# An output bias written into PSUM by ScalarE in place of products with ones, and attention masks held in bf16

## The chip, the core and the metric

One NeuronCore of a Trainium2 chip runs the whole program. The metric is the device time of one launch in microseconds (us), as the median of three runs. TensorE is called PE in the views, its weight loads PEld, VectorE DVE, ScalarE ACT, GpSimd POOL and SyncE SP.

## The reference, cut to what matters

128 graphs of 128 nodes with 512 features each go through two layers. `adj` (int32) masks both attentions.

```python
# layer 0: attention with 8 heads of 64, then a projection with a bias
q, k, v = x @ Wq + bq, x @ Wk + bk, x @ Wv + bv
logits = where(adj > 0, q @ k.T / 8, -1e9)          # per head
out = softmax(logits) @ v
x = layernorm(x + relu(out @ Wo + bo))
# layer 1: graph attention with one head
Wh = x @ W1
e = leaky(Wh @ a1 + (Wh @ a2).T)                    # one column plus one row
attention = softmax(where(adj > 0, e, -9e15))
x = layernorm(x + leaky(attention @ Wh))
```

The change touches the `bo` of layer 0 and the masks of both layers.

## The kernel before, in words

**Turns.** The loop at L914 makes one turn `t` for each graph, software-pipelined: turn `t` computes the scores of graph `t` (`Softmax.scores`, L496), applies the softmax to them, and attends for graph `t-1` (`attend`, L573). Graphs are taken in pairs for the projections: in an odd turn, `LayerZero` (L649) multiplies the pair `(t-3)//2` by Wo; in an even turn, `LayerOne` (L739) multiplies a pair by W1. Groups of four graphs are multiplied by Wq, Wk and Wv (`group_product`, L349), in 21 steps that are spread over four turns by the calls `group()`. In turn `t` an `Edge` (L760) does the attention of layer 1 for graph `t-7`. The order on every engine is the order in which the code issues, since the schedule is manual (L840). The last four graphs, and all that is still in flight, follow a list written out by hand (`PLAN`, L1124), in which `a0.p1` is the method `p1` of the job `a0`; `a0`, `a1` and `a2` are the last three LayerZero pairs, `e0` to `e10` edges and `s0` to `s3` softmaxes.

**Pair products.** All the large products are made by Strassen's method: seven products `p1` to `p7` (numbered 0 to 6 as `n`) of half size go into three PSUM banks, called y, w and x, and the blocks of the result are read out of these as soon as they are complete (`strassen`, L294; the order is at L284). Each product is two multiplications in float32 (`multiply`, L444, one for each half of the contraction) of a 128-column stationary operand with 256 moving columns; the trace shows every such multiplication in float32 as two instructions, so a product is a row x4. For LayerZero, before the first product into bank y (`p1`) and the first into bank w (`p5`), one more multiplication (L447) puts the bias into the bank: `ones` (96 x 128, bf16) by half of `bias_rows` (96 x 512, bf16), in which the rows 0, 32 and 64 hold three bf16 parts that add up to `bo`. The second half of these rows holds the difference of the two halves of `bo`, as Strassen's sums need it. `load_bias` (L173) makes these rows in the turns at the start: one subtraction, and three times a cast, a copy of one row and a subtraction, all on VectorE, as "chores" that the calls `group()` take from a list.

**PSUM.** The banks of `psum()` (L98) rotate through five buffers of one tag (L95): a tile takes the buffer of the tile allocated five places earlier and has to wait until that one has been read. A turn allocates eight: the two score tiles `lg`, `p_e` (`Edge.turn`, L773), `p_y`, `p_w`, `p_x`, `p_oT` (`attend`) and `p_h` (`Edge.product`, L800). The banks of the group products are three others (L356).

**Masks.** `load_mask` fetches the int32 block, `mask_float` (L477) casts it to float32 on ScalarE, and `mask` (L482) turns it into 0 or -1e30 on VectorE. It is added to the scores (`Softmax.add`, L508, one instruction for each `lg` tile), and seven turns later `Edge.turn` transposes it on TensorE into `p_e` (L777), after a transpose of a broadcast column of Wh (L776).

Of the kernel before, what the change touches and what calls it, by code (L numbers as in the profile page):

```python
# [8 lines left out]
F32 = mybir.dt.float32  # L9
# [15 lines left out]
def kernel(  # L25
# [53 lines left out]

    nc = tc.nc
    B, P, D = x.shape
    assert P == 128 and B % GROUP == 0 and D == 4 * P
# [13 lines left out]
    def psum(name):  # L98
        return ps_mm.tile([P, D], F32, name=name, tag="mm")


    ident = const.tile([P, P], F32, name="ident")
    make_identity(nc, ident)
    mhalf = const.tile([P, 1], F32, name="mhalf")
    nc.gpsimd.memset(mhalf, -0.5)

# [45 lines left out]
    w1 = const.tile([P, 7, 2, HALF + 1], F32, name="w1")  # L152
    wv = dram.tile([7, P, 2, HALF], F32, name="wv", bufs=1)

    bias_rows = const.tile([96, D], BF16, name="bias_rows")
    nc.gpsimd.memset(bias_rows, 0.0)
    ones = const.tile([96, P], BF16, name="ones")
    nc.gpsimd.memset(ones, 1.0)

    def load_wv():  # L160

# [9 lines left out]
        return [write(0)] + ops + [write(n) for n in (4, 5, 1, 6, 3, 2)]  # L171

    def load_bias():  # L173

        bo_b = work.tile([P, D], F32, name="bo_b", tag="y")
        nc.sync.dma_start(bo_b, bo.partition_broadcast(P))
        ops = [lambda: nc.vector.tensor_sub(bo_b[:, HALF:], bo_b[:, HALF:], bo_b[:, :HALF])]

        def part(n):
            def split():  # L180
                row = slice(32 * n, 32 * n + 1)
                part = work.tile([P, D], BF16, name="b_part", tag="z")
                nc.vector.tensor_copy(part, bo_b)
                nc.vector.tensor_copy(bias_rows[row, :], part[row, :])
                nc.vector.tensor_sub(bo_b, bo_b, part)

            return split

        return ops + [part(n) for n in range(3)]

    def load_w1():

# [246 lines left out]
    def pair_product(xs, w, add, bias=None, home=None, bank=None):  # L439


        width = w.shape[-1]

        def multiply(p, n, start):  # L444
            if start and bias is not None and n in (0, 4):
                cols = slice(0, HALF) if n == 0 else slice(HALF, D)
                nc.tensor.matmul(  # L447
                    p[:, :width], ones, bias[:, cols], start=True, stop=True, skip_group_check=True
                )
                start = False  # L450
            for kc in range(2):
                nc.tensor.matmul(  # L452
                    p[:, :width],
                    xs()[n][:, kc, :],
                    w[:, PLACE[n], kc, :],
                    start=start and kc == 0,
                    stop=True,
                    skip_group_check=True,
                )

        def read_out(name, p, o):
            t = home(name) if home else work.tile([P, HALF + 1], F32, name=f"pr_{name}")
            nc.scalar.copy(t[:, :width], p[:, :width])  # L463
            return t[:, :width]

        return strassen(
            bank or (lambda role: psum(f"p_{role}")),
            multiply,
            read_out,
            lambda h, o, p, t: add(h, o, p[:, :width], t),  # L470
        )

    def load_mask(b):
        MF[b] = small.tile([P, P], I32, name="adj", bufs=2)
# [1 line left out]

    def mask_float(b):  # L477
        a = MF[b]
        MF[b] = small.tile([P, P], F32, name="mf", bufs=9)
        nc.scalar.copy(MF[b], a)  # L480

    def mask(b):  # L482
# [2 lines left out]
    class Softmax:  # L485
# [10 lines left out]
        def scores(self):  # L496
            b = self.b
            q, k = (a[b // GROUP, b % GROUP // 2] for a in (Q, K))
            cols = slice(b % 2 * P, (b % 2 + 1) * P)
            self.lg = [psum(f"lg{r}").rearrange("p (c k) -> p c k", c=NC) for r in range(2)]  # L500
            for c in range(NC):
                for r in range(2):
                    rows = slice(r * HD, (r + 1) * HD)
                    nc.tensor.matmul(  # L504
                        self.lg[r][:, c, :], q[rows, c, cols], k[rows, c, cols], start=True, stop=True
                    )

        def add(self, r):  # L508
# [64 lines left out]
        def attend(self):  # L573

            b = self.b
            v = V[b // GROUP, b % GROUP // 2][:, b % 2, :]
            self.oT = psum("p_oT").rearrange("p (c q) -> p c q", c=NC)
            for c in range(NC):
                for r in range(2):
                    h = 2 * c + r  # L580
                    nc.tensor.matmul(  # L581
                        self.oT[r * HD : (r + 1) * HD, c, :],
                        v[:, h * HD : (h + 1) * HD],
                        self.paT[:, r * NC + c, :],
                        start=True,
                        stop=True,
                    )

        def copy(self):
# [59 lines left out]
    class LayerZero:  # L649


        def __init__(self, pair, homes=None, on_scalar=False):
            self.pair = pair
            self.on_scalar = on_scalar
            self.homes = homes or {}
            self.y = self.norms = None
            self.d = {}
            pieces = pair_product(lambda: pair_blocks(OT, pair, "oS")[0], wo, self.add, bias_rows)
            for name, piece in pieces.items():
                setattr(self, name, piece)  # L660

# [98 lines left out]
    class Edge:  # L760
# [12 lines left out]
        def turn(self):  # L773
            self.s = WH[self.b][:, :, HALF : HALF + 1]
            self.p = psum("p_e").rearrange("p (c k) -> p c k", c=NC)
            nc.tensor.transpose(self.p[:, 0, :], self.s[:, 0, :].to_broadcast([P, P]), ident)  # L776
            nc.tensor.transpose(self.p[:, 1, :], MF.pop(self.b), ident)  # L777

        def add(self):
            self.e = self.tile("e", [P, P], small, 1)  # L780
# [68 lines left out]
    zero = {}  # L849
# [64 lines left out]
    for t in range(-3, END):  # L914
# [28 lines left out]

        last, sm = sm, Softmax(t) if on(t) else none
        sm.scores()
        while later:
            later.pop(0).go_back()
        if t < 3:
# [173 lines left out]
    for n in range(6):  # L1122
# [12 lines left out]
        v.c12 s2.exp.2.3 el.store s3.scores e0.maxima s2.exp.6.7 s1.fetch sl.attend e0.exp  # L1135
        s2.exp.4.5 e0.divide e1.turn b1.p5 s0.transpose sl.copy e0.product m3.cast
        s2.reciprocals.1 sl.sum.0 e1.add m3.mask b1.p2 s3.add.0 s2.divide.6.7 sl.sum.1
        s1.transpose s2.divide.4.5 a0.p1 sl.sum.2 b1.t2 e0.copy sl.sum.3 b1.p7 b1.c11 a0.t0
        s3.add.1 s2.exp.0.1 a0.p6 s3.reduce b1.t3 s0.attend a0.t2 e0.residual s3.exp.0.1 a0.p7
        s3.exp.6.7 a0.p5 b1.c22 x2.x a0.t3 s2.reciprocals.0 e1.maxima s3.exp.2.3 a0.p4  # L1140
        s2.divide.0.1 a0.c22 b1.p3 e1.exp s3.reciprocals.0 s2.divide.2.3 a0.c21 a0.p3 e1.divide
        s3.divide.0.1 s2.store a0.stats.1 e1.product s3.divide.2.3 b1.c12 a0.rstd.1 s3.exp.4.5
        s1.attend e0.stats e1.copy e3.turn s3.reciprocals.1 e0.rstd b1.p4 s0.copy e1.residual
        s2.fetch s1.copy a0.p2 e1.stats x3.x s3.divide.6.7 a0.c11 s1.sum.0 a0.c12 s3.divide.4.5
        s1.sum.1 e3.add s3.store a0.stats.0 s1.sum.2 e0.apply a1.p1 b1.c21 e1.rstd e0.store
        e3.maxima a0.apply.1 e2.turn a1.p2 a1.t0 a0.store.1 s2.transpose e3.exp a0.rstd.0 a1.p6
        e2.add s3.fetch e1.apply e2.maxima a1.p5 s1.sum.3 a1.t2 a0.apply.0 e3.divide a1.p7
        e1.store e2.exp a1.c11 a0.fetch.1 s2.attend e2.divide a1.t3 a1.c22 a1.p4 s2.copy
        a0.store.0 s3.transpose a1.p3 a1.c21 a1.stats.1 s3.attend a0.transpose.1 a0.fetch.0
        a1.rstd.1 e3.product s3.copy a1.c12 e2.product e3.copy a1.stats.0 s3.sum.0 a2.p2  # L1150
        a1.apply.1 s3.sum.1 e3.residual e2.copy a1.store.1 a2.p5 s3.sum.2 a0.transpose.0 a2.p1
# [63 lines left out]
```

## Time and profile before

| what | value |
|---|---|
| median of three runs (lowest, highest) | 2464.59 us (2463.76, 2466.36) |
| the profiled execution, its own time | 2466.47 us |
| its span, first to last instruction | 2464.4 us |
| granted TensorE clock | 0.996 of full |
| busy share of the span: PE, DVE, ACT, POOL | 98%, 73%, 58%, 32% |
| instructions | 43800 |
| L447, bias into bank y and into bank w | 64 and 64 |
| L777, transpose of the mask | 128 |
| L480, cast of the mask on ACT | 128, 289 ns at the median |
| L483, mask to 0 or -1e30 on DVE | 128, 185 ns at the median |

The profile is of one execution. A row of the timeline gives the start from the beginning of the span, the duration, the engine, the line of the code, the operation, the tiles (output, arrow, inputs), the shapes and a count, and in brackets how long the engine had been idle before it and what ended that. [...] several are under way at once. How long one holds up the next is therefore read from start to start.

### The profile page before, as it was taken

How to read it: one execution, taken by the hardware profiler on the slowest of the kernel's cores; microseconds unless marked ns; L12 is line 12 of the kernel's file. 1: busy time of each engine (PE TensorE's matmuls, PEld its weight loads, DVE VectorE, ACT ScalarE, POOL GpSimd, SP SyncE). 2: the span in 40 equal slices, each digit the busy share in tenths (PEclk: the TensorE clock that was granted, in tenths of full speed). 3: DMA queues.
4: the chain of work that ended last, by engine and by line, in shares of the span. 5: the costliest groups of instructions: out<-in, count | busy, mean ns of one | idle time of the engine just before them, and what ended most of it. 6: DMA issues, size and time to landing. Idle time of an engine off the chain costs nothing.

```text
span 2464.4 us, 43800 instructions
## 1 busy us (share of the span) xinstructions
PE 2425.7 (98%) x13713; PEld 1996.7 (81%) x13713; DVE 1807.8 (73%) x3739; ACT 1441.2 (58%) x5206; POOL 788.8 (32%) x1197
## 2 busy tenths in 40 slices
PE   8899999999999999999999999999999999999997
PEld 6688888888888888888888888888888888888874
DVE  5667777777777777777777777777777777777788
ACT  2555556556655655565566556555655665566574
POOL 2223333323233233333232332333332323323325
PEclk9999999999999999999999999999999999999998
DMA  6544544445545445444444454444454444544443
GB/s 191 180 137 149 160 150 155 162 143 156 162 142 170 140 157 164 147 155 162 142 158 156 150 166 145 154 163 147 156 162 141 159 154 151 167 145 153 154 150 112
DMA packets 351112, 379.92 MB, mean 154 GB/s; under 512 B 38936, under 2 KB 255008, under 8 KB 350880
## 3 DMA queue, kind: packets, MB, share of 16 engines
q1 hardware_dynamic: 350016, 376.07, 47.4%
q8 instruction: 110, 1.80, 0.3%
q10 hardware_dynamic: 864, 1.05, 0.2%
q14 instruction: 122, 1.00, 0.1%
HBM read 240.91 MB, written 136.05 MB: 153 GB/s over the span
## 4 chain that ended last, share of the span: by engine, by line
PE 93%; DVE 2%; issue 2%; POOL 1%; ACT 1%; DMA 1%; SPq 0%; DVEq 0%; POOLq 0%; ACTq 0%
PE st_y L366 27%; PE p_y L452 17%; PE st_w L366 14%; PE p_w L452 9%; PE st_x L366 7%; PE lg L504 5%; PE p_oT L581 5%; PE p_x L452 4%; PE p_h L803 4%; PE p_e L776 1%; PE p_e L777 1%; ACT pa L533 0%; POOL rstd L632 0%; ACT pa L547 0%; PE p_y L447 0%
## 5 line engine op out<-in xcount | busy, mean ns | idle before, releaser
L630 POOL TENSOR_SCALAR ve<-mv 128x1 f32<-128x1 f32 x256 | 69.2, 270 | 1336.5 <-DVE mv L626 1328.8
L533 ACT ACTIVATE pa<-pa,nmax 128x128 f32<-128x128 f32 x1008 | 392.7, 393 | 42.5 <-DVE nmax L522 34.4
L547 ACT ACTIVATE pa<-pa,rs 128x128 f32<-128x128 f32 x1008 | 331.4, 395 | 30.0 <-DVE rs L543 30.0
L594 ACT ACTIVATE oT<-p_oT,b_cols 128x128 f32<-128x128 f32 x504 | 142.9, 366 | 197.3 <-PE p_w L452 194.7
L513 DVE TENSOR_TENSOR pa<-lg,mf 128x512 f32<-128x512 f32 x252 | 161.8, 683 | 97.9 <-PE lg L504 95.4
L343 ACT COPY st_t<-st_y 128x512 f32<-128x512 f32 x192 | 110.5, 576 | 155.5 <-PE st_y L366 155.5
L504 PEld LDWEIGHTS lg<-kT,qT 64*128 64x128 f32 x2048 | 124.2, 187 | 91.9 <-issue 91.9
L533 ACT ACTIVATION_READ_ACCUMULATOR pa<-pa,nmax 128x1 f32 x1008 | 191.4, 190 | 0.0
L632 POOL TENSOR_TENSOR rstd<-ve,mhalf 128x1 f32<-128x1 f32 x256 | 176.6, 690 | 21.3
L463 ACT COPY pr_t<-p_y 128x257 f32<-128x257 f32 (+1 forms) x375 | 137.1, 366 | 63.6 <-PE p_y L452 60.5
L568 DVE STREAM_TRANSPOSE paT<-paz 128x1024 f32<-128x1024 f32 x126 | 156.8, 1245 | 1.4 <-PE p_oT L581 0.4
L522 DVE TENSOR_REDUCE nmax<-pa 128x8 f32<-128x1024 f32 x126 | 153.7, 1220 | 4.4
L504 PE MATMUL lg<-kT,qT 64*128 64x128 f32 x2048 | 148.8, 285 | 0.0
L347 ACT ACTIVATE st_t<-st_y,b_cols 128x256 f32<-128x256 f32 x192 | 80.5, 470 | 114.8 <-PE st_y L366 114.8
L581 PEld LDWEIGHTS p_oT<-paT,v 128*64 128x64 f32 x2016 | 107.5, 136 | 45.1 <-issue 39.5
L581 PE MATMUL p_oT<-paT,v 128*64 128x128 f32 x2016 | 137.9, 279 | 3.2 <-DVE paT L568 3.2
L781 ACT ACTIVATE e<-p_e,wh 128x128 f32<-128x128 f32 x117 | 43.2, 369 | 156.3 <-PE p_e L777 156.3
L751 DVE TENSOR_TENSOR wh<-p_w,pr_t 128x257 f32<-128x257 f32 x122 | 51.5, 422 | 110.4 <-PE p_w L452 63.6
L452 PE MATMUL p_y<-w,x1T 128*128 128x257 f32 x496 | 128.5, 381 | 2.5 <-ACT wk L463 1.7
L452 PE MATMUL p_y<-wo,oS 128*128 128x256 f32 x504 | 129.5, 379 | 0.4 <-ACT pr_t L463 0.4
L452 PE MATMUL p_y<-wo,oT 128*128 128x256 f32 x504 | 129.5, 379 | 0.0
L366 PE MATMUL st_y<-wv_n,xS 128*128 128x256 f32 x512 | 124.6, 386 | 3.7 <-ACT pa L547 2.8
(205 smaller groups left out, 6021.1 us busy)
## 6 DMA issues: line engine op xcount, KB each, us to landing
pa_dram<-pa SPq DMA_DIRECT2D x126, 512.0 KB, 2.6
paz<-pa_dram SPq DMA_DIRECT2D x504, 128.0 KB, 2.7
wv_n<-wv SPq DMA_DIRECT2D x224, 256.0 KB, 2.9
x<-in_x_dram SPq DMA_DIRECT2D x128, 256.0 KB, 2.9
x_dram<-x SPq DMA_DIRECT2D x128, 256.0 KB, 2.3
xz<-x_dram SPq DMA_DIRECT2D x512, 64.0 KB, 2.0
xz<-in_x_dram SPq DMA_DIRECT2D x496, 64.0 KB, 2.2
out_dram<-z SPq DMA_DIRECT2D x120, 256.0 KB, 2.5
```

Source lines behind the costliest of these rows:

```text
L366: nc.tensor.matmul(p[:, m, :], lhs, rhs, start=start and m == 0 and kc == 0, stop=True, skip_group_check=True,)
L452: nc.tensor.matmul(p[:, :width], xs()[n][:, kc, :], w[:, PLACE[n], kc, :], start=start and kc == 0, stop=True, skip_group_check=True,)
L463: nc.scalar.copy(t[:, :width], p[:, :width])
L504: nc.tensor.matmul(self.lg[r][:, c, :], q[rows, c, cols], k[rows, c, cols], start=True, stop=True)
L513: nc.vector.tensor_add(by_head[:, r * NC : (r + 1) * NC], self.lg[r].rearrange("p c (b k) -> p c b k", b=4), mf.unsqueeze(1).to_broadcast( ...
L522: nc.vector.tensor_reduce(self.nmax, by_head, AX.XY, ALU.max, negate=True)
L533: nc.scalar.activation(self.pa[:, :, h, :], self.pa[:, :, h, :], AF.Exp, bias=self.nmax[:, h : h + 1], accum_out=self.sums[:, h : h + 1],)
L547: nc.scalar.activation(self.pa[:, :, h, :], self.pa[:, :, h, :], AF.Copy, scale=self.rs[:, h : h + 1])
L568: nc.vector.transpose(self.paT.rearrange("p h (a i) -> p a h i", i=32), self.paz.rearrange("p a (h k) -> p a h k", k=32),)
L581: nc.tensor.matmul(self.oT[r * HD : (r + 1) * HD, c, :], v[:, h * HD : (h + 1) * HD], self.paT[:, r * NC + c, :], start=True, stop=True,)
L594: nc.scalar.activation(OT[pair][:, c, h * P : (h + 1) * P], self.oT[:, c, :], AF.Identity, bias=b_cols[:, 1, c : c + 1],)
L632: nc.gpsimd.tensor_tensor(self.r, ve, mhalf, ALU.pow)
```

## The change

The rows `bias_rows`, the tile `ones` and the two products with it go. `bo`, broadcast to 128 partitions in float32, stays in SBUF (`bo_b`), with the same subtraction of its halves. Two new pieces, `by` and `bw`, each allocate one bank (y or w) and have ScalarE copy 128 x 256 values of `bo_b` into it; `p1` and `p5` then accumulate onto it (no multiplication of theirs has `start`), and only `p2`, into bank x, starts afresh. In the loop the two pieces are issued in odd turns straight after the scores, ahead of `Edge.turn`; in `PLAN` each stands immediately ahead of its `p1` or `p5`. The other users of the same buffers (scores, `attend`, `turn`) set `start` on the first multiplication of a bank alone. The mask is cast to bf16 instead of float32, and its transpose in `Edge.turn` is a plain multiplication with a bf16 identity, which VectorE copies from the float32 identity at the start.

```diff
+    ident_b = const.tile([P, P], BF16, name="ident_b")
+    nc.vector.tensor_copy(ident_b, ident)
...
-    bias_rows = const.tile([96, D], BF16, name="bias_rows")
-    nc.gpsimd.memset(bias_rows, 0.0)
-    ones = const.tile([96, P], BF16, name="ones")
-    nc.gpsimd.memset(ones, 1.0)
+    bo_b = const.tile([P, D], F32, name="bo_b")
...
     def load_bias():
-        bo_b = work.tile([P, D], F32, name="bo_b", tag="y")
         nc.sync.dma_start(bo_b, bo.partition_broadcast(P))
-        ops = [lambda: nc.vector.tensor_sub(bo_b[:, HALF:], bo_b[:, HALF:], bo_b[:, :HALF])]
-        def part(n):
-            def split():
-                row = slice(32 * n, 32 * n + 1)
-                part = work.tile([P, D], BF16, name="b_part", tag="z")
-                nc.vector.tensor_copy(part, bo_b)
-                nc.vector.tensor_copy(bias_rows[row, :], part[row, :])
-                nc.vector.tensor_sub(bo_b, bo_b, part)
-            return split
-        return ops + [part(n) for n in range(3)]
+        return [lambda: nc.vector.tensor_sub(bo_b[:, HALF:], bo_b[:, HALF:], bo_b[:, :HALF])]
...
         def multiply(p, n, start):
-            if start and bias is not None and n in (0, 4):
-                cols = slice(0, HALF) if n == 0 else slice(HALF, D)
-                nc.tensor.matmul(
-                    p[:, :width], ones, bias[:, cols], start=True, stop=True, skip_group_check=True
-                )
-                start = False
+            start = start and (bias is None or n == 1)
...
+        ready = {}
+        def biased(role, half):
+            def run():
+                ready[role] = psum(f"p_{role}")
+                nc.scalar.copy(ready[role][:, :HALF], bias[:, half * HALF : (half + 1) * HALF])
+            return run
+        def get_bank(role):
+            if role in ready:
+                return ready.pop(role)
+            return bank(role) if bank else psum(f"p_{role}")
...
+        if bias is not None:
+            pieces["by"], pieces["bw"] = biased("y", 0), biased("w", 1)
...
-        MF[b] = small.tile([P, P], F32, name="mf", bufs=9)
+        MF[b] = small.tile([P, P], BF16, name="mf", bufs=9)
...
-            nc.tensor.transpose(self.p[:, 1, :], MF.pop(self.b), ident)
+            nc.tensor.matmul(
+                self.p[:, 1, :],
+                MF.pop(self.b),
+                ident_b,
+                start=False,
+                stop=True,
+                skip_group_check=True,
+            )
...
         sm.scores()
+        if t % 2 == 1 and on(t - 3):
+            zero[(t - 3) // 2].by()
+            zero[(t - 3) // 2].bw()
...
-        s1.transpose s2.divide.4.5 a0.p1 sl.sum.2 b1.t2 e0.copy sl.sum.3 b1.p7 b1.c11 a0.t0
+        s1.transpose s2.divide.4.5 a0.by a0.p1 sl.sum.2 b1.t2 e0.copy sl.sum.3 b1.p7 b1.c11 a0.t0
```

The other five places of `PLAN` are changed in the same way (`a0.bw`, `a1.by`, `a1.bw`, `a2.bw`, `a2.by`).

More of the change, by code (lines that the diff above doesn't have):

```diff
@@ L464, in read_out @@
             return t[:, :width]
-        return strassen(
-            bank or (lambda role: psum(f"p_{role}")),
+        ready = {}
[8 more added lines that the diff above has]
+            return bank(role) if bank else psum(f"p_{role}")
+        pieces = strassen(
+            get_bank,
             multiply,
@@ L471, in pair_product @@
         )
+        if bias is not None:
+            pieces["by"], pieces["bw"] = biased("y", 0), biased("w", 1)
+        return pieces
     def load_mask(b):
@@ L504, in scores @@
                     nc.tensor.matmul(
-                        self.lg[r][:, c, :], q[rows, c, cols], k[rows, c, cols], start=True, stop=True
+                        self.lg[r][:, c, :],
+                        q[rows, c, cols],
+                        k[rows, c, cols],
+                        start=c == 0,
+                        stop=True,
+                        skip_group_check=True,
                     )
@@ L584, in attend @@
                         self.paT[:, r * NC + c, :],
-                        start=True,
+                        start=c == 0,
                         stop=True,
+                        skip_group_check=True,
                     )
@@ L657, in __init__ @@
             self.d = {}
-            pieces = pair_product(lambda: pair_blocks(OT, pair, "oS")[0], wo, self.add, bias_rows)
+            pieces = pair_product(lambda: pair_blocks(OT, pair, "oS")[0], wo, self.add, bo_b)
             for name, piece in pieces.items():
@@ L776, in turn @@
             nc.tensor.transpose(self.p[:, 0, :], self.s[:, 0, :].to_broadcast([P, P]), ident)
-            nc.tensor.transpose(self.p[:, 1, :], MF.pop(self.b), ident)
+            nc.tensor.matmul(
[3 more added lines that the diff above has]
+                start=False,
+                stop=True,
+                skip_group_check=True,
+            )
         def add(self):
@@ L1137 @@
         s2.reciprocals.1 sl.sum.0 e1.add m3.mask b1.p2 s3.add.0 s2.divide.6.7 sl.sum.1
-        s1.transpose s2.divide.4.5 a0.p1 sl.sum.2 b1.t2 e0.copy sl.sum.3 b1.p7 b1.c11 a0.t0
+        s1.transpose s2.divide.4.5 a0.by a0.p1 sl.sum.2 b1.t2 e0.copy sl.sum.3 b1.p7 b1.c11 a0.t0
         s3.add.1 s2.exp.0.1 a0.p6 s3.reduce b1.t3 s0.attend a0.t2 e0.residual s3.exp.0.1 a0.p7
-        s3.exp.6.7 a0.p5 b1.c22 x2.x a0.t3 s2.reciprocals.0 e1.maxima s3.exp.2.3 a0.p4
+        s3.exp.6.7 a0.bw a0.p5 b1.c22 x2.x a0.t3 s2.reciprocals.0 e1.maxima s3.exp.2.3 a0.p4
         s2.divide.0.1 a0.c22 b1.p3 e1.exp s3.reciprocals.0 s2.divide.2.3 a0.c21 a0.p3 e1.divide
@@ L1144 @@
         s2.fetch s1.copy a0.p2 e1.stats x3.x s3.divide.6.7 a0.c11 s1.sum.0 a0.c12 s3.divide.4.5
-        s1.sum.1 e3.add s3.store a0.stats.0 s1.sum.2 e0.apply a1.p1 b1.c21 e1.rstd e0.store
+        s1.sum.1 e3.add s3.store a0.stats.0 s1.sum.2 e0.apply a1.by a1.p1 b1.c21 e1.rstd e0.store
         e3.maxima a0.apply.1 e2.turn a1.p2 a1.t0 a0.store.1 s2.transpose e3.exp a0.rstd.0 a1.p6
-        e2.add s3.fetch e1.apply e2.maxima a1.p5 s1.sum.3 a1.t2 a0.apply.0 e3.divide a1.p7
+        e2.add s3.fetch e1.apply e2.maxima a1.bw a1.p5 s1.sum.3 a1.t2 a0.apply.0 e3.divide a1.p7
         e1.store e2.exp a1.c11 a0.fetch.1 s2.attend e2.divide a1.t3 a1.c22 a1.p4 s2.copy
@@ L1150 @@
         a1.rstd.1 e3.product s3.copy a1.c12 e2.product e3.copy a1.stats.0 s3.sum.0 a2.p2
-        a1.apply.1 s3.sum.1 e3.residual e2.copy a1.store.1 a2.p5 s3.sum.2 a0.transpose.0 a2.p1
+        a1.apply.1 s3.sum.1 e3.residual e2.copy a1.store.1 a2.bw a2.p5 s3.sum.2 a0.transpose.0 a2.by a2.p1
         a1.rstd.0 x5.x e2.residual b2.p1 a2.t0 a0.sum.0 a1.apply.0 a1.fetch.1 a2.p6 a2.c11
```

## The prediction

> **What bounds the kernel now.** I read the page first: shares of busy time, then the chain that ended last.
>
> ```profile
> PE 2425.7 (98%) x13713; PEld 1996.7 (81%) x13713; DVE 1807.8 (73%) x3739; ACT 1441.2 (58%) x5206; POOL 788.8 (32%) x1197
> ...
> PE 93%; DVE 2%; issue 2%; POOL 1%; ACT 1%; DMA 1%; SPq 0%; DVEq 0%; POOLq 0%; ACTq 0%
> ```
>
> TensorE is busy for 98% and makes 93% of the chain. The table of TensorE's waits, asked for 100 to 2360 us, has four entries, 5.1 us in all, each met once and all before 116 us. So in the loop nothing is waited for: eight turns take 150.64 us in every one of the 13 stretches that I measured by the starts of the score products. There a change is worth what it takes from or adds to TensorE's own stream; only in the first 116 us and after 2400 us do other engines set the time. The stream of one odd turn, TensorE's timeline:
>
> ```profile
> 1213.56 0.27 PE L776 MATMUL p_e<-ident,wh 128*128 128x128 f32 x1
> 1213.66 0.27 PE L777 MATMUL p_e<-ident,mf 128*128 128x128 f32 x1
> 1213.77 0.28 PE L447 MATMUL p_y<-bias_rows,ones 96*128 96x256 bf16 x1
> 1213.89 1.03 PE L452 MATMUL p_y<-wo,oT 128*128 128x256 f32 x4
> 1214.75 0.27 PE L447 MATMUL p_w<-bias_rows,ones 96*128 96x256 bf16 x1
> 1214.86 1.03 PE L452 MATMUL p_w<-wo,oS 128*128 128x256 f32 x4
> ```
>
> The rows overlap, so a product's price is not its 0.27 us but the step to the next start: 0.12 and 0.11 us here. Over all 128 bias products the step is 111 to 114 ns, 113 at the median; after L777 it is 109 ns.
>
> [...] load rows of L452 (float32) last 190 ns at the median, those of L447 (bf16) 98. [...] the nearest rows here (L463, PSUM to SBUF, 128x256) have 366 ns. I use the trace's.
>
> **The change, part by part.**
>
> *Bias products out of TensorE.* 128 x 113 ns = 14.5 us, of which 122 in the loop, 13.8 us. The steps around them stay: 216 ns for a float32 product whether a bias product or another follows, 109 after L777.
>
> *Two copies on ScalarE in each odd turn.* Each about 0.37 us; successive ScalarE rows overlap by 0.1, so both take 0.64 us. Where they land, from ScalarE's timeline:
>
> ```profile
> 1210.74 0.58 ACT L809 COPY z<-p_h 128x512 f32<-128x512 f32 x1 [0.27 <-PE p_h L803]
> 1213.97 0.37 ACT L781 ACTIVATE e<-p_e,wh 128x128 f32<-128x128 f32 x1 [2.65 <-PE p_e L777]
> 1214.95 0.37 ACT L463 COPY pr_t<-p_y 128x256 f32<-128x256 f32 x1 [0.61 <-PE p_y L452]
> ```
>
> They stand between the first two rows, in 2.65 us of idle time: done by 11.32 + 0.64 = 1211.96, while TensorE wants bank y at 1213.77. That is 1.8 us of cover; behind them in ScalarE's queue are L781, which has to wait for TensorE anyway, and the exponentials. Cost nothing; without cover 0.64 us in each of 61 odd turns, 39 us. I count a gain from ScalarE as excluded.
>
> *Banks.* With `by` and `bw` ahead of `p_e`, an odd turn allocates lg, lg, y, w, e, x, oT, h instead of lg, lg, e, y, w, x, oT, h. Five places back: `by` now waits for the last turn's x, `bw` for its oT, both read long before (oT by ScalarE itself, earlier in its queue). `p_e` waits for the last p_h, whose copy (L809) ends 2.2 us or more ahead of L776 in every loop turn. `p_h` now waits for bank y of its own turn, last read by VectorE at L666: over all odd turns that read ends 0.91 us or more ahead of L803, and 0.23 us goes from this as TensorE gets faster, which leaves 0.68. The next turn's scores wait for bank w as before. All cost nothing; a VectorE later by 0.7 us would begin to show at L803.
>
> *Mask product in bf16.* [...] But the product after it needs a float32 load, and the trace starts each load 2 ns after the product before it has started, so loads run one ahead only. [...] its row is 92 ns longer than a bf16 one. So the step stays between 92 + 2 and 113 ns: from 1.9 us gained (128 x 15 ns) to 0.5 us lost. I take 0[...]. `start` on fewer products changes no count of instructions: 0. The cast to bf16 on ScalarE and the mask on VectorE have the same elements and both engines wait for TensorE: 0. No row shows an addition with mixed types (L513, 683 ns now, two a turn); a gain reaches nobody, and a loss shows only from 3.5 us a turn on, since VectorE idles 1.48 and 1.39 us between them and the reads of bank y, on top of the 0.68: 0.
>
> *Setup.* The bf16 identity is one VectorE copy while VectorE waits until 4.68 us for x: hidden. Two POOL memsets go, also hidden. But the splitting of bo into rows goes too, and that was in somebody's way. VectorE, then TensorE:
>
> ```profile
> 56.39 0.43 DVE L183 CAST b_part<-bo_b 128x512 bf16<-128x512 f32 x1
> ...
> 60.08 0.69 DVE L185 TENSOR_TENSOR bo_b<-bo_b,b_part 128x512 f32<-128x512 f32 x1
> 60.69 1.28 DVE L513 TENSOR_TENSOR pa<-lg,mf 128x512 f32<-128x512 f32 x2
> ...
> 63.14 1.23 DVE L568 STREAM_TRANSPOSE paT<-paz 128x1024 f32<-128x1024 f32 x1
> ```
>
> ```profile
> 64.43 1.09 PE L581 MATMUL p_oT<-paT,v 128*64 128x128 f32 x16 [0.94 <-DVE paT L568]
> 65.82 1.96 PE L366 MATMUL st_y<-xS,wq 128*128 128x256 f32 x8 [0.30 <-ACT st_t L347]
> 71.53 1.99 PE L366 MATMUL st_y<-xT,wq 128*128 128x256 f32 x8 [0.73 <-ACT st_t L347]
> 78.80 1.09 PE L581 MATMUL p_oT<-paT,v 128*64 128x128 f32 x16 [1.82 <-DVE paT L568]
> ```
>
> Nine operations hold the mask additions up by 4.3 us, and VectorE has no gap from there to the paT that TensorE waits for. Without them paT is ready near 62.0 (its DMA lands at 60.8) where TensorE comes at 63.5, and the exponentials start 4 us earlier: the waits of 0.94, 0.30 and 0.73 go, 2.0 us. The fourth depends on the store and fetch of the softmax: divisions end near 68 instead of 70.5, the fetch lands near 74.6, VectorE has paT near 76.1, against 75.0 at which TensorE would come. What is late next is this DMA: 0.7 of 1.82 goes. Later waits (1.11, 0.48, 2.85 us up to 112 us) hang on the same chain and move with it. Gain 2.6 us; bounds 0 (a later wait takes it back) and 3.8 (all four).
>
> *Tail.* Here `by` and `bw` stand straight ahead of their products, with ScalarE's queue ahead of them. The worst, `a1.by`, comes after `e0.apply`:
>
> ```profile
> 2400.02 0.84 ACT L641 ACTIVATE z<-z,shift,rstd 128x512 f32<-128x512 f32 x1
> ```
>
> Its copy ends near 2401.1, while `p1` starts its work at 2399.05 now: 2.1 us late. Of this 1.07 us is covered, since TensorE idled so long before `p6` at 2402.22; `p7`, now at 2404.89, would then be 0.8 late behind `a1.bw`. `a0.by` and `a0.bw` cost 0.2 and 0.4 by the same reading, inside that same cover; `a2.bw` about 0.5, against an idle 0.88 us at 2415.57. I take a net 0.7 us lost, the six products saved there included; bounds 0.7 gained (all covered) and 2.5 lost (no cover).
>
> *Sum.* -13.8 - 2.6 + 0.7 + 0 = -15.7 us. The profiled execution took 2466.47 us, 2.1 around its span of 2464.4; the sum makes it 2450.8 (span 2448.7). It lies 1.9 above the median of the runs, 2464.59, and the saving is the same for both: **2448.9 us**.
>
> **The rivals.** *The mask product shrinks with its columns* (load not in the way): 128 x 53 ns = 6.8 us more, 2442.1. For it: bf16 loads and products are shorter. Against it: the float32 load behind it. *Only the stream gets shorter*: the start's 2.6 us is taken back by the next wait and the tail has no cover: -13.8 + 2.5, 2453.3. For it: at 105 to 116 us four other waits follow. *Slower: the copies become the wait of each odd turn.* If the bank's release reaches ScalarE only with TensorE's group step ahead of L776 (rows end at 1213.7), the copies are done at 1214.35 instead of 1211.96, bank y is late by about 0.7 us against a saving of 0.226, and 61 x 0.47 = 29 us makes 2493. It decides from 1.8 + 0.23 = 2.0 us of lateness on. Against it: nothing that these banks held is still read then. That the products with ones stay in some form is excluded by the diff.
>
> **How the numbers follow.** Forecast 0.74; shrinking mask 0.07; stream alone 0.12; late copies 0.07, of which 0.03 near break-even. Lower end: -13.8 - 0.7 - 3.8 - 1.9 = -20.2, 2444.4; upper: -13.8 + 0 + 0.5 + 2.5 = -10.8, 2453.8; runs lie up to 1.8 above their median, so I end the range at 2444.0 and 2455.0. Left out are the shrinking mask and the late copies, 0.14, and a little of the rest. 0.2%, 4.9 us, is about what a measurement of this kernel can tell from no change. Faster 0.93, same 0.03, slower 0.04.
>
> **What would show it.** Eight turns at 150.64 - 8 x 0.113 = 149.74 us; 128 ScalarE rows from bo_b, in loop turns ahead of L781's idle time; the mask product's step near 109 ns; TensorE's 0.94 us wait at 64 us gone; new waits of TensorE for ScalarE only after 2385 us. Wrong if eight turns are not near 149.7, or if TensorE waits for p_y or p_h in the loop.

## The result and the profile after

The changed kernel took **2455.38 us** at the median (four runs, 2454.73 to 2456.53) beside 2464.55 us for the kernel before (four runs, 2463.76 to 2466.36): a ratio of 0.9962, with a 95% interval of 0.9945 to 0.9980 (each experiment below has its ratio and, in brackets, the same interval). That is 9.2 us faster, where 15.7 had been forecast. The profiled execution after took 2454.73 us with a span of 2452.6. The page, first the shares of busy time, then the chain by engine:

```profile
PE 2412.3 (98%) x13585; PEld 1989.0 (81%) x13585; DVE 1802.0 (73%) x3731; ACT 1478.2 (60%) x5334; POOL 789.8 (32%) x1195
...
PE 93%; issue 1%; DMA 1%; DVE 1%; ACT 1%; POOL 1%; SPq 1%; DVEq 0%; POOLq 0%; ACTq 0%
```

TensorE has 128 instructions and 13.4 us of work less, ScalarE 128 more and 37 us more, and TensorE makes 93% of the chain as it did before. `bo` is zero in the inputs of all runs: they show what the copies cost in time, not that a product accumulated onto a copy gives the right sum. The page hides where the difference lies. So I cut both traces at two marks, the first score product of graph 8 and that of graph 124:

| stretch | before, us | after, us | difference | forecast |
|---|---|---|---|---|
| start, to graph 8 | 174.65 | 172.31 | -2.3 | -3.3 |
| loop, graph 8 to 124 | 2186.09 | 2173.60 | -12.5 | -13.1 |
| end, from graph 124 | 103.66 | 106.73 | +3.1 | +0.7 |
| sum (span) | 2464.4 | 2452.6 | -11.8 | -15.7 |

In the forecast column six of the 122 bias products (0.7 us) stand with the start, where they are. The two profiled executions differ by 11.8 us, the medians by 9.2.

**The loop.** TensorE's timeline of a turn, after (in the changed kernel L784 is the transpose of Wh, L785 the mask product, L435 a pair product):

```profile
1223.45 0.27 PE L784 MATMUL p_e<-ident,wh 128*128 128x128 f32 x1
1223.56 0.22 PE L785 MATMUL p_e<-ident_b,mf 128*128 128x128 bf16 x1
1223.62 1.09 PE L435 MATMUL p_y<-w,x1T 128*128 128x257 f32 x4
1224.54 1.03 PE L435 MATMUL p_w<-w,x1S 128*128 128x257 f32 x4
```

Eight turns take 149.75 us (150.64 before). The bias products are gone, and nothing waits in their place. But the mask product's step is now 56 ns, not 109; instead the pair product after it takes 0.92 us from start to start, where the next of its kind takes 0.87. For its first instruction alone the step is 272 ns instead of 219: 56 + 272 = 328 = 109 + 219.

**The start.** TensorE, after (L588 is `attend`):

```profile
63.20 1.09 PE L588 MATMUL p_oT<-paT,v 128*64 128x128 f32 x16
...
78.81 1.97 PE L588 MATMUL p_oT<-paT,v 128*64 128x128 f32 x16 [4.40 <-DVE paT L575]
```

At 63.20 it is 1.23 us earlier than before and waits for nothing; near 71.5 us it is 2.5 us ahead. Then it stands for 4.40 us and goes on at 78.81, where the kernel before went on at 78.80: all the lead is gone at one instruction. The DMA issues on SP's queue say why, first before, then after (L553 and L560 store the softmax, L559 and L566 fetch it back):

```profile
66.44 0.43 SPq L195 DMA_DIRECT2D a_b<-in_L_gnn_a_dram  x1
70.58 0.34 SPq L553 DMA_DIRECT2D pa_dram<-pa  x1
73.23 1.75 SPq L559 DMA_DIRECT2D paz<-pa_dram  x4
```

```profile
66.80 0.43 SPq L183 DMA_DIRECT2D a_b<-in_L_gnn_a_dram  x1
67.34 0.36 SPq L560 DMA_DIRECT2D pa_dram<-pa  x1
73.01 1.75 SPq L566 DMA_DIRECT2D paz<-pa_dram  x4
```

The store is issued 3.24 us earlier, but its fetch only 0.22 us earlier. From issue to landing the store took 5.6 us, where it takes 2.6 in most of the run. Just ahead of it stand the loads of layer 1's weights, 1.5 MB issued from 63.0 to 66.8 us. VectorE's mask additions felt it too; they need the buffer that the store reads:

```profile
73.08 1.29 DVE L520 TENSOR_TENSOR pa<-lg,mf 128x512 f32<-128x512 f32 x2 [4.14 <-DMA pa_dram<-pa]
```

**The granted clock.** Busy time by stretch, before and then after (the columns are the stretch, its length, busy time and instructions of PE, PEld, DVE, ACT and POOL, the granted TensorE clock, the DMA share and GB/s):

```profile
78.00:84.00 6.00, 5.20 (x45) 4.32 (x46) 3.70 (x14) 4.86 (x20) 1.01 (x2) 1.00 0.45 146
112.00:121.00 9.00, 8.06 (x23) 6.11 (x24) 3.79 (x6) 3.45 (x11) 5.03 (x7) 0.62 0.68 221
```

```profile
78.00:85.00 7.00, 6.19 (x34) 4.67 (x36) 4.70 (x15) 5.00 (x20) 2.00 (x3) 0.54 0.45 148
106.00:122.00 16.00, 11.50 (x72) 8.83 (x72) 10.83 (x20) 8.85 (x34) 9.06 (x10) 1.00 0.69 210
2387.00:2392.00 5.00, 4.33 (x13) 3.45 (x14) 4.62 (x12) 3.71 (x10) 4.36 (x11) 0.66 0.84 305
```

The kernel before had its low clock in 112 to 121 us, after its wait of 2.85:

```profile
112.27 2.40 PE L366 MATMUL st_y<-wv_n,xS 128*128 128x256 f32 x8 [2.85 <-ACT pa L547]
```

There it cost 9 x 0.38 = 3.4 us of full clock. The changed kernel has it in 78 to 85 (7 x 0.46 = 3.2 us), after the wait of 4.40, and once more in the end (5 x 0.34 = 1.7 us), at a place where the kernel before had none. Only in the last 13 us have both of them a low clock, after a wait of 3.15 us in each (13.3 us from that product to the end before, 13.2 after), so this makes no difference between them.

The values between 0.5 and 1 are means of stretches that are low in part. Cut at 0.1 us, the clock is 0.50 from 113.6 to 120.5 us before, and from 77.6 to 84.4 and from 2388.4 to 2391.9 after: 6.9, 6.8 and 3.5 us. So the start has as much low clock before as after, 3.4 us of full clock each; its loss is not a matter of the clock between these two profiles.

**The end.** TensorE, then ScalarE, after (L456 is the new copy, L649 the apply):

```profile
2377.95 1.13 PE L435 MATMUL p_w<-wo,oS 128*128 128x256 f32 x4 [1.00 <-ACT p_w L456]
2387.67 1.39 PE L435 MATMUL p_y<-wo,spare 128*128 128x256 f32 x4 [2.01 <-ACT p_y L456]
2401.47 1.10 PE L435 MATMUL p_w<-wo,oS 128*128 128x256 f32 x4 [0.56 <-POOL oS L264]
```

```profile
2386.47 0.86 ACT L649 ACTIVATE z<-z,shift,rstd 128x512 f32<-128x512 f32 x1
2387.18 0.43 ACT L456 COPY p_y<-bo_b 128x256 f32<-128x256 f32 x1
```

In the kernel before, TensorE had these waits there:

```profile
2402.22 1.10 PE L452 MATMUL p_y<-wo,spare 128*128 128x256 f32 x4 [1.07 <-ACT pr_t L463]
2404.89 1.10 PE L452 MATMUL p_y<-wo,spare 128*128 128x256 f32 x4 [0.59 <-POOL shift L637]
2415.57 1.14 PE L452 MATMUL p_y<-w,x1T 128*128 128x257 f32 x4 [0.88 <-DVE x1T L245]
```

The wait that the forecast foresaw is there, 2.01 us for `a1.by` behind `e0.apply` (forecast 2.1), with 0.17 and 1.00 for pair `a0`. What follows it was not foreseen: the low clock, 0.66 in the mean of 2387 to 2392 us.

### The profile page after: what moved, and what is told of

It reads as the page before. It is cut to its first block, busy times and chain, and to the rows that moved or that the text cites. A ratio compares the mean times of both kernels' runs of the same rounds, so it can differ in the third digit from the quotient of the medians.

```text
span 2452.6 us, 43635 instructions
## 1 busy us (share of the span) xinstructions
PE 2412.3 (98%) x13585; PEld 1989.0 (81%) x13585; DVE 1802.0 (73%) x3731; ACT 1478.2 (60%) x5334; POOL 789.8 (32%) x1195
## 4 chain that ended last, share of the span: by engine, by line
PE 93%; issue 1%; DMA 1%; DVE 1%; ACT 1%; POOL 1%; SPq 1%; DVEq 0%; POOLq 0%; ACTq 0%
PE st_y L354 27%; PE p_y L435 17%; PE st_w L354 14%; PE p_w L435 9%; PE st_x L354 7%; PE lg L506 5%; PE p_oT L588 5%; PE p_x L435 4%; PE p_h L818 4%; PE p_e L784 1%; DMA wv_n<-wv 0%; SPq L228 0%; ACT pa L540 0%; POOL rstd L640 0%; PE p_e L785 0%
## 5 line engine op out<-in xcount | busy, mean ns | idle before, releaser
L588 PEld LDWEIGHTS p_oT<-paT,v 128*64 128x64 f32 x2016 | 108.2, 137 | 46.8 <-issue 39.9
L588 PE MATMUL p_oT<-paT,v 128*64 128x128 f32 x2016 | 138.8, 280 | 5.0 <-DVE paT L575 5.0
L435 PE MATMUL p_y<-w,x1T 128*128 128x257 f32 x496 | 131.6, 388 | 1.6 <-ACT wk L446 1.5
L435 PE MATMUL p_y<-wo,oT 128*128 128x256 f32 x504 | 132.7, 386 | 0.2 <-ACT p_y L456 0.2
L435 PE MATMUL p_y<-wo,oS 128*128 128x256 f32 x504 | 129.4, 379 | 0.0
L435 PE MATMUL p_y<-w,x1S 128*128 128x257 f32 x496 | 128.0, 380 | 0.0
```

The costliest lines, as they stand in the source:

```text
L435: nc.tensor.matmul(p[:, :width], xs()[n][:, kc, :], w[:, PLACE[n], kc, :], start=start and kc == 0, stop=True, skip_group_check=True,)
L588: nc.tensor.matmul(self.oT[r * HD : (r + 1) * HD, c, :], v[:, h * HD : (h + 1) * HD], self.paT[:, r * NC + c, :], start=c == 0, stop=True, ...
```

## The experiments

Theory: the loop gave what was forecast, the mask nothing; the end lost more because of waits for copies and the low clock that the longest of them brings; the start lost because the store stands behind weight loads. Rivals: the mask gives something that is hidden; the loss in the end has nothing to do with the copies; the clock alone sets the start.

**The changed kernel again (r_same).** No edit.

> The changed kernel again, unaltered. Theory: the loop is fixed (eight turns at 149.75 us in nearly every stretch), and what differs between executions lies in the first 125 us and after 2385 us, where TensorE waits and its granted clock drops to about half for some 5 us at a time; so the median is 2455 to 2456 and the profile shows the drop at 79 to 85 us again or at another place. Rival (the loop itself varies, by a stray DMA or copy that is late): stretches of eight turns scatter by 0.3 us or more.

2456.68 us beside 2466.22: 0.9957 (0.9945 to 0.9970). The start took 172.59, the loop 2173.13 and the end 106.62 us, so the three differences repeat. The low clock came in the end again (0.66 in 2387 to 2392), but at the start in two places, behind waits of 3.19 and 2.71 us:

```profile
77.00:82.00 5.00, 4.80 (x27) 3.67 (x29) 3.03 (x13) 3.86 (x16) 0.68 (x1) 0.66 0.48 157
110.00:119.00 9.00, 7.66 (x21) 5.76 (x22) 4.15 (x7) 4.56 (x15) 4.53 (x6) 0.62 0.70 231
```

The loop in the profile after was longer by 0.47: TensorE waited once for a load of `wv_n` near 1460 us, and here it doesn't. The 116 bias products of the loop are thus worth 12.96 us, 0.112 each.

**The mask alone taken back to float32 (x1_mask_f32).** To hold memory, `bo_b` is bf16, so `bo` is rounded.

```diff
-        MF[b] = small.tile([P, P], BF16, name="mf", bufs=9)
+        MF[b] = small.tile([P, P], F32, name="mf", bufs=9)
...
+            nc.tensor.transpose(self.p[:, 1, :], MF.pop(self.b), ident)
```

> The changed kernel with its masks back in float32 and transposed as before (bo_b is held in bf16 to make room, which rounds bo). Theory (the float32 weight load behind the mask product sets the step, whatever the product takes): the step after the mask product is 109 ns instead of 56, the next product gives the 53 ns back, eight turns stay at 149.75 us, total within 1.5 us of the changed kernel, 2454 to 2457. Rival (bf16 masks are part of the gain): eight turns at 150.17, total 6.8 us above the changed kernel, 2462.

2454.91 beside 2466.22: 0.9951 (0.9937 to 0.9965). TensorE's rows have the old steps again, 0.11 us after the mask product:

```profile
1224.85 0.27 PE L786 MATMUL p_e<-ident,wh 128*128 128x128 f32 x1
1224.96 0.27 PE L787 MATMUL p_e<-ident,mf 128*128 128x128 f32 x1
1225.07 1.03 PE L437 MATMUL p_y<-w,x1T 128*128 128x257 f32 x4
```

Eight turns take 149.75 and the loop 2173.13 us, as in r_same; the end takes 107.10. The bf16 mask is thus worth nothing in the changed kernel; this is shown.

**No bias at all (x2_no_bias).** `by`, `bw` and their six places in `PLAN` go; `bo` is left out.

```diff
-            pieces = pair_product(lambda: pair_blocks(OT, pair, "oS")[0], wo, self.add, bo_b)
+            pieces = pair_product(lambda: pair_blocks(OT, pair, "oS")[0], wo, self.add)
```

> The changed kernel without any bias in layer 0's projection: no copies into PSUM, no products with ones (bo is left out). Theory (in the loop the copies are covered, in the last pairs they stop TensorE): eight turns stay at 149.75 us, TensorE's waits of 0.17, 1.00 and 2.01 us after 2370 us are gone with the half clock that follows, total 2.5 to 4 us below the changed kernel, 2451.5 to 2453. Rival (the copies cost something in each odd turn): eight turns fall below 149.6. Rival (the end loses its time to other waits): the last 107 us from the scores of graph 124 on stay as long as in the changed kernel.

2453.96 beside 2466.22: 0.9951 (0.9939 to 0.9964). The loop is 2173.13, the same to 0.01 us as with the copies: in the loop they cost nothing. In the end the waits for copies and the low clock are gone (granted 1.00 in 2370 to 2392 us), but the end is 105.61, only 1.1 shorter, less than expected. TensorE now waits 1.43 us for a read-out on ScalarE (`pr_t`), 1.54 for `x1T` on VectorE and 1.26 for `wk` on ScalarE. This suggests that a good part of the end is a chain of other engines that reappears wherever TensorE is relieved. The start is 170.91 here, with a low clock of 3.4 us alone (79.4 to 82.8), and none behind a wait of 2.62 us at 111.82.

**The mask product ahead of the transpose (x3_mask_first).** The mask product sets `start`, and the float32 transpose comes between it and the pair product.

```diff
-            nc.tensor.transpose(self.p[:, 0, :], self.s[:, 0, :].to_broadcast([P, P]), ident)
             nc.tensor.matmul(
                 self.p[:, 1, :],
                 MF.pop(self.b),
                 ident_b,
-                start=False,
+                start=True,
                 stop=True,
                 skip_group_check=True,
             )
+            nc.tensor.transpose(self.p[:, 0, :], self.s[:, 0, :].to_broadcast([P, P]), ident)
```

> The changed kernel with the two multiplications of Edge.turn exchanged: the bf16 mask product ahead of the float32 transpose. Theory (the float32 load behind the mask product is what hides its gain): now the transpose, with its shorter load, follows the mask product [...]; each turn is 53 ns shorter, eight turns 149.33 us, total 6.5 us below the changed kernel, 2449. Rival (going from bf16 to float32 costs a fixed 53 ns, or TensorE keeps a least distance between products): eight turns stay at 149.75 and the total at 2455.

2450.61 beside 2466.22: 0.9932 (0.9920 to 0.9945). TensorE's timeline:

```profile
1223.84 0.22 PE L784 MATMUL p_e<-ident_b,mf 128*128 128x128 bf16 x1
1223.90 0.28 PE L792 MATMUL p_e<-ident,wh 128*128 128x128 f32 x1
1224.01 1.03 PE L435 MATMUL p_y<-w,x1T 128*128 128x257 f32 x4
...
1224.88 1.03 PE L435 MATMUL p_w<-w,x1S 128*128 128x257 f32 x4
```

The steps are 56, 112 and 219 ns, the pair product takes 0.87 again, and eight turns take 149.33, 0.42 less (8 x 53 ns). So the gain of the shorter mask product is seen or hidden by what stands behind it, and neither a fixed price of the change from bf16 to float32 nor a least distance between products is the reason, since both orders have the change. That it is the float32 load of the pair product which hides the gain fits the load rows (190 ns for a pair product, 137 for the transpose), but is argued from them. The start of this profile is 175.59 us, with low clock in 77.0 to 83.9 and 111.2 to 121.5.

**The loads of W1 behind the store (x5_late_w1).** They are issued at the end of turn 1, the work on them a turn later.

```diff
-        if t == 1:
-            late_chores = load_w1()
-        if t in (0, 2):
+        if t in (0, 3):
...
+        if t == 1:
+            late_chores = load_w1()
```

> The changed kernel with the load of W1 issued at the end of turn 1 instead of at its start, behind the store and fetch of that turn's softmax; its VectorE chores start a turn later. Theory (the store of the softmax lands at 73 us before and after the change, because W1 and the row of a, 1.5 MB on the same queue, are ahead of it): the store issued at 67.3 us lands near 70, the paT that TensorE waits for comes 2 to 3 us earlier, its wait of 3.2 to 4.4 us at 78 us falls below 1.5 and the half clock behind it does not come; total 3 to 5 us below the changed kernel run beside before, by which the ratio to before falls to 0.9945. Rival (the store itself takes 5.6 us whatever is ahead of it): wait and total as in the changed kernel.

2456.20 beside 2465.07: 0.9966 (0.9953 to 0.9978), and the start 176.87, 4.6 longer. The first half is as expected: the store, issued at 66.89, is followed by its fetch at 69.52, and TensorE waits 1.22 instead of 4.40. So the loads ahead of it were what delayed the store. But 10 us later, TensorE and ScalarE:

```profile
75.21 1.09 PE L588 MATMUL p_oT<-paT,v 128*64 128x128 f32 x16 [1.22 <-DVE paT L575]
85.05 1.57 PE L435 MATMUL p_y<-wo,oT 128*128 128x256 f32 x4 [3.81 <-ACT p_y L456]
```

```profile
83.94 0.30 ACT L482 CAST mf<-adj 128x128 bf16<-128x128 int32 x1 [4.64 <-DMA adj<-in_adj_dram]
```

The load of `adj` now stands behind W1 on SP's queue (issued at 78.85), the cast of the mask waits for it, and the copy of the bias stands behind the cast on ScalarE. That is the hazard of the change: TensorE's product now waits for whatever is ahead of the copy in ScalarE's queue.

**The copies earlier in the end (x4_early_copies).** Each stands several entries ahead of its product in `PLAN`, `a1.by` ahead of `e0.apply`. Shortened:

```diff
-s2.divide.6.7 sl.sum.1 s1.transpose s2.divide.4.5 a0.by a0.p1
+s2.divide.6.7 a0.by sl.sum.1 s1.transpose s2.divide.4.5 a0.p1
-a0.c12 s3.divide.4.5 s1.sum.1 e3.add s3.store a0.stats.0 s1.sum.2 e0.apply a1.by a1.p1
+a0.c12 a1.by s3.divide.4.5 s1.sum.1 e3.add s3.store a0.stats.0 s1.sum.2 e0.apply a1.p1
```

> The changed kernel with by and bw of the last three pairs moved ahead in the written-out order, as far as the rotation of the banks allows (bw of the first and of the second pair and both of the third straight behind the allocation before them; by of the second pair only behind c12, which frees its bank at 2386.4 us). Theory (ScalarE's queue ahead of the copies is the wait): of TensorE's 3.2 us of waits for these copies about 1.2 are left, all for by of the second pair; with a wait that short the half clock may not come; 1.5 to 3 us less from the scores of graph 124 to the end than the changed kernel's 106.6. Rival (the banks come free late): waits as before the move.

2454.61 beside 2465.07: 0.9960 (0.9947 to 0.9974). The end is 104.83, 1.9 shorter. One wait for a copy is left, and the clock is 1.00 in 2375 to 2392 us:

```profile
2385.72 1.13 PE L435 MATMUL p_y<-wo,spare 128*128 128x256 f32 x4 [0.79 <-ACT p_y L456]
```

For the end this is as expected.

**Products with ones in the end only (x6_tail_ones).** Loop as changed; the last three pairs as before, with `bias_rows` made at the end of turn 1.

```diff
-            pieces = pair_product(lambda: pair_blocks(OT, pair, "oS")[0], wo, self.add, bo_b)
+            pieces = pair_product(lambda: pair_blocks(OT, pair, "oS")[0], wo, self.add,
+                                  None if on_scalar else bo_b, rows=bias_rows if on_scalar else None)
```

> The changed kernel with the old products with ones for the last three pairs alone (the splitting of bo is done between turns 1 and 2, where VectorE is idle). Theory: TensorE waits for no copy after 2370 us; from the scores of graph 124 to the end it takes some 103.7 us, as in the kernel before, or 3 us less than the changed kernel's 106.7; eight turns stay at 149.75 us. Rival (the end loses its time otherwise): over 106.

2453.07 beside 2465.07: 0.9952 (0.9939 to 0.9964). The end is 104.53, 2.2 shorter, with no wait for a copy and the clock at 1.00 in 2384 to 2392; it stays 0.9 above that of the kernel before, with the same bias instructions in it. TensorE's longest waits there, ahead of the last 13 us:

```profile
2386.91 1.10 PE L461 MATMUL p_y<-wo,spare 128*128 128x256 f32 x4 [1.32 <-ACT pr_t L472]
2400.45 1.14 PE L461 MATMUL p_y<-w,x1T 128*128 128x257 f32 x4 [1.35 <-DVE x1T L253]
2410.29 1.14 PE L461 MATMUL p_y<-w,x1T 128*128 128x257 f32 x4 [1.26 <-ACT wk L472]
```

In the kernel before they were 1.07, 0.88 and 0.99, and the idle times of the end add up to 9.8 us here against 8.7 there. So of 3.1 us, about 2.2 come from the copies (waits and clock). The other 0.9 does not: it is time in which TensorE waits longer for the same results of ScalarE and VectorE. Why these come no earlier stays open.

**Three of these together (x7_best_ones).** Mask product first, W1 late, products with ones in the end.

> Three of these together: mask product ahead of the transpose, W1 loaded later, products with ones in the last three pairs. If they are independent: 6.5 for the exchange, 3 to 5 for the load, 3 for the end, 12.5 to 14.5 us below the changed kernel, 2442; eight turns at 149.33 us. If the waits at the start and at the end are given back by each other's successors: only the exchange shows, 2449.

2448.35 beside 2465.07: 0.9936 (0.9924 to 0.9949). Loop 2167.14 and end 105.55, but start 177.03: the late W1 costs what it did above, and the parts don't add up to 2442.

**TensorE kept busy ahead of the long wait (x10_fill).** Eight products into a bank that nobody reads, ahead of `attend` in turn 2.

```diff
+            if t == 2:
+                f = psum("fill")
+                for _ in range(8):
+                    nc.tensor.matmul(
+                        f[:, :HALF], wq[:, 0, 0, :P], wq[:, 0, 0, :], start=True, stop=True,
+                        skip_group_check=True,
+                    )
```

> The changed kernel with eight multiplications of 256 columns in float32 (3.5 us of work, written to a bank that nobody reads) ahead of the p_oT of turn 2, where TensorE otherwise waits 3.2 to 4.4 us for paT. Theory (a wait of that length brings TensorE's clock down to about half for some 5 us, and that is where the time saved at 64 to 72 us goes): the wait falls below 1.3 us, no half clock at 79 to 85, the scores of graph 8 start 1.5 to 3 us earlier than in the executions of the changed kernel that have the drop (172.3, 172.6), so at 170 or 171. Rival (the half clock comes for another reason): it stays, and as much is gained as lost, 172 to 174.

2455.65 beside 2465.04: 0.9964 (0.9950 to 0.9979). TensorE's rows, and the stretches:

```profile
78.90 1.09 PE L588 MATMUL p_oT<-paT,v 128*64 128x128 f32 x16 [1.33 <-DVE paT L575]
107.46 3.38 PE L354 MATMUL st_x<-wv_n,xT 128*128 128x256 f32 x8 [2.62 <-DMA wv_n<-wv]
```

```profile
79.00:85.00 6.00, 6.00 (x49) 4.79 (x50) 3.66 (x16) 4.64 (x16) 1.90 (x3) 1.00 0.42 154
107.00:111.00 4.00, 3.54 (x10) 2.42 (x12) 1.80 (x9) 3.88 (x19) 1.30 (x1) 0.61 0.58 157
```

The idle time before `attend` is cut from 4.40 to 1.33 us, and the clock stays at 1.00. So at this place the idle time brings the low clock; that part is shown. But the start is 172.28, not the 170 or 171 that was expected: the lead is handed over to a wait of 2.62 us for `wv_n` (0.5 in the profile after), with a low clock of its own. That the clock alone sets the start is thus excluded.

It has a part in it, though, as the profiles show whose start is that of the changed kernel, or nearly: with 3.4 us of half clock the start is 170.91 (x2_no_bias), with 6.8 to 6.9 us 172.19 and 172.31 (x8_first_early and the profile after), with 10.3 to 10.4 us 172.59 to 173.71 (r_same, x4_early_copies, x1_mask_f32), and with 17.2 us 175.59 (x3_mask_first). This is a correlation over seven profiles.

**Mask first and early copies (x8_first_early), and these with the fill (x11_all).**

> The changed kernel with the mask product ahead of the transpose and the copies of the last three pairs earlier. If both are independent: 6.5 us for the exchange and 1.8 for the end (104.8 against 106.6), 8 us below the changed kernel, a ratio to before of 0.9925; eight turns at 149.33 us.

2450.57 beside 2465.04: 0.9937 (0.9924 to 0.9950). The loop takes 2167.14 and the end 105.88 us, with a new wait of 2.19 us for `x1T` on VectorE at 2394.91 and half clock behind it, from 2395.3 to 2398.8.

> The same with the filling products of turn 2 as well. If they save the half clock there: 1.5 to 3 us more, 10 us below the changed kernel, a ratio to before of 0.9915.

2450.22 beside 2465.04: 0.9939 (0.9926 to 0.9952). The start takes 173.38 and the end 107.1 us, with a wait of 2.16 us for `spare` on VectorE. Neither beats the mask product first alone by more than the intervals. In the end the waits that were taken away came back elsewhere (2.19 and 2.16 us).

**The kernel before again (b_same).** No edit.

> The kernel before again, unaltered, for a second profile. Theory (half clock follows only waits of 2 us and more): its wait of about 1.8 us at 78 us brings no drop, the one of 2.8 us at 112 us does as in the first profile; scores of graph 8 at 174 to 175 us, eight turns at 150.64, last part 103.7. If the drops are free of the waits, one may be at 79 us here too, and then the start is 2 us longer.

2465.94 beside 2465.04: 1.0002 (0.9993 to 1.0010). The loop takes 2186.09 us as in the first profile and the end 103.5, but the start 175.39, which is 0.7 longer. The pattern at the start is the same: after the wait of 1.82 at 78.44 the clock is 1.00, around the wait of 2.75 for `wv_n` that ends at 111.82 it falls to 0.50:

```profile
111.00:121.00 10.00, 8.50 (x19) 6.32 (x20) 3.46 (x7) 4.10 (x13) 4.78 (x7) 0.50 0.65 215
```

## Why the prediction was right in kind and wrong in size

**Bias products out of TensorE: right.** 0.112 us each in the loop where 0.113 was taken.

**Copies in the loop: right.** 128 copies, at 382 and 378 ns at the median (bank y, bank w) where 366 was taken from the reads in the other direction, and no wait. Without them (x2_no_bias) the loop is the same. The banks that moved by five places cost nothing either.

**Mask in bf16: the value 0 was right, its picture was not, so the 0 is in part luck.** The forecast held the mask product's own step at 109 ns because of the load behind it, and named this step as a sign. The rows gave it 94 to 113 ns; the 109 within this was my estimate alone. The step fell to 56, and the 53 ns came back in the product after it. The sum is what counts, and x1_mask_f32 and x3_mask_first show it from both sides. The additions of a bf16 mask take as long as before (684 ns each, 683 before), as forecast. With the order of two instructions exchanged the rival that I gave 0.07, a product whose step shrinks, becomes true: its 53 ns, an estimate when it was made, are the difference of the 109 and 56 ns measured since.

**Start: forecast -2.6, measured -1.7** (2.3 less the 0.7 of its bias products). The waits of 0.94, 0.30 and 0.73 us went as the step said. It failed at "the fetch lands near 74.6": the store landed not 2.6 us but 5.6 us after its issue, because 1.5 MB of weight loads stood ahead of it. I had moved the store to an earlier time and left its duration as it was; x5_late_w1 shows it short again when the loads are moved away. And I had named DMA as what is late next, but not asked what a longer wait of TensorE does to its clock: there is now a low clock at 78 us, in r_same and other profiles beside the one near 112 and in the profile after in its place. The size of this miss, 0.9 us, is no more than what profiles of one start differ by (0.7 in the kernel before, more where the low clock is longer); that the step failed is shown by the wait of 4.40 us where 1.1 (1.82 - 0.7) had been forecast.

**End: forecast +0.7, measured +3.1: the largest miss inside the trace.** Its waits were right in sum. The copies brought 0.17, 1.00 and 2.01 us (0.4, 0.2 and 2.1 had been read for `a0.bw`, `a0.by` and `a1.by`), and POOL's `oS` 0.56. In exchange the idle times of 1.07 and 0.59 us went and that of 0.88 fell to 0.18, so the cover was real. TensorE's idle times in the end add up to 8.69 us before and 10.34 after: 1.65 more, and less the 0.68 of six products this would be +1.0. What failed is that a wait was priced at its length: behind the 2.01 us the clock was at half for 3.5 us, 1.7 us of full clock that stood in no term. It was no accident of one profile: the low clock follows the same wait (2.0 to 2.1 us) in r_same, at 0.66 in the mean of 2387 to 2392 us as here, and in x3_mask_first, x5_late_w1 and x10_fill, where the row x4 of `p_x` behind it takes 1.91 to 2.02 us instead of 1.03. That leaves 0.4 of the 3.1, which is not traced further. x4_early_copies and x6_tail_ones, in which the waits for copies and the low clock go wholly or for the most part, get 1.9 and 2.2 back. What is left in x6_tail_ones, 0.9, is longer waits for the same results of ScalarE and VectorE; x2_no_bias, in which other waits take the place of those removed, points the same way. That their chain sets the pace there is argued, not shown.

**From the profile to the median: 2.6 us.** "The saving is the same for both" did not hold: the profiled executions differ by 11.8 us, the medians by 9.2. The profile before lay 1.9 above its median, the one after 0.7 below. Each run also lists its mean granted clock. Of 46 executions of the kernel before that are listed with it, 35 have 0.997 (median 2465.13 us) and six 0.995 (2467.39). Of the nine of the changed kernel, one has 0.997 (2452.98), two have 0.996 (2454.73 and 2455.94), five 0.995 (median 2456.53) and one 0.994 (2458.61). At equal clock the saving is thus 11 to 12 us, as between the two profiles; the saving of the medians is smaller, as the changed kernel mostly runs at a lower clock than the one before. An estimate from the traces: one stretch of 3.4 us at half clock takes 1.7 of 2455 us, or 0.0007, from the mean, so 0.997 and 0.995 are about three such stretches apart, while the two profiles differ by one of them (6.9 us of half clock before, 10.3 after, the last 13 us apart). Two more stretches, up to 1.7 us each, would make up the 2.6. That is a correlation: x10_fill raised the clock to 0.996 and 0.997 and did not get faster. Whether the lower clock or the waits that come with it take the time in those executions, and at which place, stays open.

Together: 0.9 at the start, 0.6 in the loop (0.5 of it the stray wait), 2.4 at the end and 2.6 from profile to median make the 6.5 us between 2448.9 and 2455.4. The rival "only the stream gets shorter" (2453.3) had the nearest time, and its reasons, a next wait at the start and an end without cover, are the nearest to what happened.

## What to carry to other kernels

A product moved from TensorE, busy for 98% of the span, to another engine's copy gave its whole step back here (0.112 us) where the copy ended 2.1 us or more ahead of the product, as in the loop; where the copy was held up by what stood before it in the queue, TensorE waited for it, 2.01 us at most in the end and 3.81 us in x5_late_w1: ask what is in that queue. A step that is moved earlier has a new environment: look up what its DMA will stand behind (5.6 us to the store's landing here, where 2.6 had been taken), and what TensorE's longer idle time does to its clock (0.50 from 77.6 to 84.4 us, around the end of a wait of 4.40). And a shorter product may gain nothing where it stands: here the bf16 product, with a step of 56 ns instead of 109, gained only once it was put ahead of the transpose, whose load is shorter (137 against 190 ns). Look at the step of the product behind it, not at its own alone.

## What the runs showed of the hardware

- **A step can be hidden in its successor.** The bf16 product took 56 ns to the next start, and then the first instruction of the float32 pair product 272 instead of 219 ns, which is the 109 + 219 of the float32 mask again. In the other order the three steps are 56, 112 and 219.
- **The clock was either full or half, and half for 3.4 to 3.5, 6.8 to 6.9 or 10.3 us.** Cut at 0.1 us, it was 1.00 or 0.50 in the profiles before and after, but for the slices at the edges. Ahead of the last 13 us it was half for 6.9 us from 113.6 in the kernel before, for 6.8 from 77.6 and 3.5 from 2388.4 in the profile after, and for 10.3 from 110.8 in b_same, whose window of 111 to 121 above is at 0.50. What sets these lengths is not shown. Half clock came with waits of 1.93 (x6_tail_ones, at 107.21), 2.01, 2.19, 2.62, 2.75, 2.85 and 4.40 us. None came with any wait up to 1.82 alone (in x5_late_w1 it is there behind one of 1.06, at 113.59, but one of 2.27 had ended at 111.44), and none with 2.12 (x7_best_ones, at 45.25), 2.32 (the profile after, at 112.92, in the stretch 106 to 122 above), 2.62 (x2_no_bias, at 111.82) and 3.04 us (x11_all, at 107.64). The first wait of each span is not counted, as the traces don't show what was ahead of it. So between 1.93 and 3.04 us some waits had half clock with them and some had not; the length of the wait alone does not decide, and what does is not shown.
- **A store's landing depended on the loads issued ahead of it**: 5.6 us behind 1.5 MB, 2.6 in most of the run, and a fetch 2.6 us after its issue (69.52 - 66.89) with those loads moved away. Whether the order on the queue or the load on the DMA engines does this, no run separates.
